# A gated state-space and channel-mix layer: a new set-up for the order of POOL's and SP's queues, D's scaling, early D products and the value weights

## The chip, the cores and the metric

One core of a Trainium2 chip runs the whole layer. The metric is the device time of one execution in microseconds (us); the time before the change is the median of three runs. All data are fp32. Engines are named as in the profile: PE is TensorE, DVE VectorE, ACT ScalarE, POOL GpSimd, SP the engine whose queue issues most transfers.

## What is computed

The input x is 4 batches of 2048 time steps of 512 channels. Six rows of modulation per batch come from a small vector c. With them the layer does this (names shortened):

```python
mod = (silu(c) @ wmod).reshape(B, 6, 1, -1)      # sa, ca, ga, sb, cb, gb
ga, gb = (sign(g) * max(abs(g), 0.25) for g in (ga, gb))
h = layernorm(x) * (1 + ca) + sa
omega = clip(softplus(h @ W_omega.T + b_omega), 1e-4, 100); d = 1 - sigmoid(h @ W_zeta.T + b_zeta)
A = omega * omega; S = 1 / (1 + DT * DT * A); F = h @ W_B.T + b_B
z, y = d*(S*z - DT*A*S*y) + F_z, d*(DT*S*z + S*y) + F_y      # over time, 64 pairs per batch
x = x + ga * (states @ C.T + h @ D.T)
h = layernorm(x) * (1 + cb) + sb
xr, xk = (mu * h + (1 - mu) * h_of_the_step_before for mu in (mu_r, mu_k))
x = x + gb * sigmoid(xr @ W_r.T) * (relu(xk @ W_k.T) ** 2 @ W_v.T)
```

## The kernel before

The sequence is cut into 32 units of 256 time steps of one batch; unit i is step range i // 4 of batch i % 4. A class `Gates` makes the inputs of the state recurrence for a unit, a function `scan` runs the recurrence for the four units of a step range together, and a class `Finish` does all the rest of a unit.

*Gates.* `load` brings x (xs, two pieces of 256 KB), `load_t` its transposed copy (xt). `norm` takes the statistics on DVE and r = 1/sqrt(var + eps) on POOL (L130). r is needed as a row on all partitions: `send` writes it to DRAM (st, L134) and `spread` reads it back broadcast (bc, L141), both on SP's queue. For the first four units `spread_now` makes the same row with a diagonal matrix and a product (L148 to L150). `project` multiplies the transposed x with the gate weights of that batch (pg, L161, one PSUM buffer), and `hand_over` scales by r on DVE (g, L169) and writes four pieces on ACT (L174). The gate weights of a batch (wgb) are the common ones scaled and centred (`shared_weights`, L512 and L517).

*Scan.* A list of closures: softening on ACT (three passes and two table loads) and on DVE (L200 to L205), eight chunk steps, joins, falls and eight state steps on DVE; then `by_batch` copies the states on ACT (L307) and moves them to y on SP's queue (L309). `take(budget)` puts the next closures of the list into the program at the place where it is called.

*Finish.* `load` brings x and its transposed copy; `shift` adds a row d0 on POOL (L337). `attend` multiplies the transposed x with D (pd, L347) and y with C (pc, L348), adds both to x on DVE (L350, L351) and takes statistics; xn is made on ACT (L363). `mix` transposes xn (L382), makes the two mixed inputs on ACT and DVE (L388, L391), first the one for the keys, with an edge added on POOL (L394). `key` (L407), `receptance` (L421) and `value` (L431) are the three big products. The D of each batch (dg) is D times the gate row ga (`d_gate`, L526, POOL), centred by `d_centre` (L533 PE, L537 DVE); C is scaled likewise (cg, L621). ga, the row of gates on all partitions, is made by `broadcast_rows`, which writes four rows to DRAM and reads them back broadcast (L505, L506, SP's queue). The value weights of a batch (wvb) are W_v scaled by gb on ACT (L670), transposed on PE (L673) and copied on ACT (L674), one piece of 128 after another.

*What sets the order.* The kernel is recorded under a manual schedule: every engine and every queue runs its own instructions in the order in which the program text issues them, each waiting for its inputs and for its buffer to be free. Tiles of pool p1 have one buffer, of p2 two, of p3 three for each tag; xs and the transposed xt share three buffers each. An instruction that waits holds everything behind it on its engine, and a transfer that waits to be issued holds its queue. The set-up is the text from the first loads to the loop over `fin`; the loop then does, for unit i, key, the gates of unit i + 8, attend and mix of unit i + 1, receptance and value, with pieces of the scan taken in between.

Of the kernel before, what the change touches and what calls it, by code (L numbers as in the profile page):

```python
# [43 lines left out]
def adaln_layer_kernel(ctx: ExitStack, tc: tile.TileContext, x, x_t, c_t, wmod, w_gate, w_b, b_gate, b_f, c_mat, d_mat,  # L44
# [64 lines left out]
    class Gates:  # L109
# [5 lines left out]

        def load(self):
            self.xs = []
            for n in range(NT):
                t = p3.tile([P, D], F32, tag="xs", name=f"xs_{self.u.tag}_{n}")
                nc.sync.dma_start(t, x[self.u.b, self.u.t0 + n * P : self.u.t0 + (n + 1) * P, :])  # L120
                self.xs.append(t)
# [21 lines left out]
        def spread_now(self, diag):  # L143
# [3 lines left out]
            for n in range(NT):  # L147
                nc.vector.tensor_scalar_mul(diag[:, ts(n, P)], ident, self.r[:, n : n + 1])  # L148
                nc.tensor.matmul(pb[:, ts(n, P)], ones, diag[:, ts(n, P)], start=True, stop=True)
# [173 lines left out]
    class Finish:  # L323
# [14 lines left out]

        def attend(self, between):
            xt, h, u = self.x, self.h, self.u  # L340
            b = u.b
            mv = p2.tile([P, NT, 2], F32, tag="mv", name=f"mv_{self.tag}")
            for n in range(NT):
                pd = ps3.tile([P, D], F32, tag="px", name=f"pd_{self.tag}_{n}")
                pc = ps3.tile([P, D], F32, tag="px", name=f"pc_{self.tag}_{n}")
                for k in range(KC):
                    nc.tensor.matmul(pd, h[:, k, ts(n, P)], dg[:, b, k, :], start=(k == 0), stop=(k == KC - 1))  # L347
                nc.tensor.matmul(pc, y_of[u.s][:, b, ts(n, P)], cg[:, b, :], start=True, stop=True)  # L348
                r = rs[:, b, u.t0 // P + n : u.t0 // P + n + 1]
                nc.vector.scalar_tensor_tensor(xt[:, n, :], pd, r, xt[:, n, :], ALU.mult, ALU.add)  # L350
# [103 lines left out]
    room = p1.tile([P, 2, KC, W], F32, tag="mixed", name="room").rearrange("p i k w -> p (i k w)")  # L454
    wraw = room[:, : KC * 4 * M].rearrange("p (k i n) -> p k i n", k=KC, i=2)
    craw = room[:, KC * 4 * M : KC * 4 * M + D]
    mag = room[:, KC * 4 * M + D :]
# [4 lines left out]
    for i, mu in enumerate((mu_r, mu_k)):  # L462
        nc.scalar.dma_start(mus[:, i, :], mu.rearrange("(k p) -> p k", p=P))
# [7 lines left out]
    gts[0].load()  # L471
    wm_ga = wmod_to(wvb[:, 1], 2)
    wm_sa = wmod_to(wvb[:, 2], 0)
    gts[0].load_t()

    dm = [
        p2.tile([P, KC // 2, D], F32, tag="y", name="dm0"),
        p1.tile([P, KC // 2, D], F32, tag="act", name="dm1"),
    ]
    for h in range(2):  # L480
        nc.scalar.dma_start(dm[h], d_mat[h * D // 2 : (h + 1) * D // 2, :].rearrange("(k p) n -> p k n", p=P))
    nc.scalar.dma_start(craw, c_mat)
# [20 lines left out]
    def broadcast_rows(dst, rows, name):  # L503
        there = dram.tile([B, D], F32, tag=name, name=name)
        nc.sync.dma_start(there, rows)  # L505
        nc.sync.dma_start(dst, there.unsqueeze(0).broadcast_to([P, B, D]))  # L506
# [17 lines left out]
    def d_gate(b):  # L524
        for h in range(2):
            nc.gpsimd.tensor_tensor(  # L526
                dg[:, b, 2 * h : 2 * h + 2, :], dm[h], ga[:, b, :].unsqueeze(1).broadcast_to([P, KC // 2, D]), ALU.mult
            )
# [12 lines left out]
    def d_rows():  # L541

        pr = ps2.tile([P, D], F32, tag="pm", name="pd0")
        for k in range(KC):
            nc.tensor.matmul(pr[:B, :], mod[:, 0, k, :], dm[k // 2][:, k % 2, :], start=(k == 0), stop=(k == KC - 1))
# [4 lines left out]
    def shift_factors():  # L550
# [7 lines left out]
        nc.vector.tensor_scalar_mul(first_f, first_f, -1.0)  # L558

# [14 lines left out]
    nc.vector.tensor_scalar_mul(mod[:, 4], mod[:, 1], 1.0 / D)  # L574
    wm_cb = wmod_to(wvb[:, 0], 4)
    gts[0].norm()
    pr = mod_rows(wm_ga, 2)
    gts[1].load()
    gts[1].load_t()
    shared_weights(0)  # L580
    sgn = p2.tile([P, D], F32, tag="r", name="sgn2")
    nc.vector.tensor_scalar(sgn[:B, :], pr[:B, :], 0.0, 2.0, ALU.is_ge, ALU.mult)
    nc.scalar.activation(mag[:B, :], pr[:B, :], AF.Abs)
# [215 lines left out]
```

## Time and profile before

| | us |
|---|---|
| median of the runs (1260.05 to 1261.03) | 1260.7 |
| the profiled execution | 1261.01 |
| its span, first to last instruction | 1259.2 |
| PE busy in the span | 1160.7 |
| DVE busy | 752.0 |
| ACT busy | 477.7 |
| POOL busy | 174.4 |

A line of the profile names the line of the kernel, the engine, the operation, and output and inputs by the program's names. In lists by time the first number is the start and the second the duration, in us; what stands in square brackets is the time that the engine idled before it and the instruction or transfer whose end came last. In lists of waits the numbers are the time in total, how often, and the longest. SPq is SP's queue, whose entries are the issue of transfers, not their landing. The clock row (PEclk) is the share of full speed that TensorE was granted.

The granted clock was 0.958 over the span. In the 300 us from the start PE is busy for 206; in each 100 us from 300 to 1200 it is busy for 100.

### The profile page before, as it was taken

Reading aid. Unit: us, or ns where it says so; the run is one execution under the profiler, and the core shown is the slowest. Engines: PE = TensorE matmul, PEld = TensorE weight load, DVE = VectorE, ACT = ScalarE, POOL = GpSimd, SP = SyncE. Lnnn points to the kernel's source line nnn. Section 1 sums busy time; section 2 is a strip of 40 time slices with the busy share of each in tenths; the row PEclk is TensorE's granted clock in tenths of the full one; section 3 lists DMA queues with packets and bytes.
Section 4 is the critical chain, followed back from the end, with each engine's and each line's share of the span. In section 5 each row is a group of like instructions: output and inputs, shape, how many; then the busy total and the mean of one; then the engine's idle time right before and its main releaser. Section 6 shows DMA issues by size and latency. Waiting matters only on the chain.

```text
span 1259.2 us, 11785 instructions
## 1 busy us (share of the span) xinstructions
PE 1160.7 (92%) x3692; PEld 674.8 (54%) x3692; DVE 752.0 (60%) x2044; ACT 477.7 (38%) x796; POOL 174.4 (14%) x254
## 2 busy tenths in 40 slices
PE   6781475899999999999999999999999999999998
PEld 2621343456655566555665555665556665555554
DVE  2557513886488647874587538863886368743332
ACT  1331534333453345434533445334533453233232
POOL 0340001111101111111111111110111011111110
PEclk9895667899999999999999999999999999999999
DMA  8565423123333333233322232323232211121100
GB/s 266 194 118 93 74 67 79 39 80 88 104 89 88 88 87 85 88 89 96 89 81 68 75 95 80 88 88 105 88 89 71 67 50 51 51 67 50 50 18 33
DMA packets 120270, 105.95 MB, mean 84 GB/s; under 512 B 15880, under 2 KB 90120, under 8 KB 119952
## 3 DMA queue, kind: packets, MB, share of 16 engines
q1 hardware_dynamic: 116064, 101.27, 29.7%
q10 hardware_dynamic: 4144, 3.94, 1.0%
q8 instruction: 29, 0.48, 0.2%
q14 instruction: 33, 0.27, 0.1%
HBM read 84.16 MB, written 16.82 MB: 80 GB/s over the span
## 4 chain that ended last, share of the span: by engine, by line
PE 86%; DVE 3%; ACT 2%; DMA 2%; issue 1%; POOL 0%; SPq 0%; DVEq 0%; ACTq 0%
PE pk_c L407 18%; PE pr_c L421 18%; PE pv_c L431 17%; PE pd_c L347 17%; PE pg L161 8%; PE pc_c L348 4%; PE pt_c L382 2%; PE pwv L673 1%; DMA bc<-st 1%; DMA xs<-in_x_dram 1%; PE pdm L533 1%; ACT wvs L670 1%; ACT wvb L674 1%; ACT f L174 0%; ACT pre L174 0%
## 5 line engine op out<-in xcount | busy, mean ns | idle before, releaser
L407 PE MATMUL pk_c<-mixed_c,wk 128*128 128x256 f32 x1024 | 228.1, 381 | 12.9 <-POOL mixed_c L394 12.9
L347 PE MATMUL pd_c<-dg,xt 128*128 128x512 f32 x512 | 232.4, 597 | 0.0
L421 PE MATMUL pr_c<-wr,mixed_c 128*128 128x512 f32 x512 | 227.0, 596 | 0.0
L431 PE MATMUL pv_c<-wvb,act_c 128*128 128x512 f32 x512 | 225.0, 592 | 0.0
L407 PEld LDWEIGHTS pk_c<-mixed_c,wk 128*128 128x128 f32 x1024 | 195.7, 191 | 53.3 <-issue 14.8
L391 DVE SCALAR_TENSOR_TENSOR mixed_c<-pt_c,prev_f,mixed_c 128x255 f32<-128x255 f32 x256 | 118.1, 482 | 122.9 <-ACT mixed_c L388 122.9
L363 ACT ACTIVATE xn_c<-x,nmr_c,rstd_c 128x512 f32<-128x512 f32 x64 | 48.6, 805 | 334.6 <-POOL nmr_c L360 334.6
L421 PEld LDWEIGHTS pr_c<-wr,mixed_c 128*128 128x128 f32 x512 | 98.2, 192 | 123.9 <-issue 123.8
L347 PEld LDWEIGHTS pd_c<-dg,xt 128*128 128x128 f32 x512 | 98.1, 192 | 110.6 <-issue 108.8
L431 PEld LDWEIGHTS pv_c<-wvb,act_c 128*128 128x128 f32 x512 | 96.7, 190 | 108.9 <-issue 106.2
L350 DVE SCALAR_TENSOR_TENSOR x<-pd_c,rs,x 128x512 f32<-128x512 f32 x64 | 47.5, 743 | 169.0 <-PE pd_c L347 168.9
L161 PE MATMUL pg<-xt,wgb 128*128 128x256 f32 x512 | 121.0, 391 | 15.4 <-DVE g L169 15.4
L388 ACT ACTIVATE mixed_c<-pt_c,mod,now_f 128x256 f32<-128x256 f32 x256 | 130.4, 561 | 11.9 <-DVE mixed_c L391 5.6
L412 ACT ACTIVATE act_c<-pk_c 128x512 f32<-128x512 f32 x64 | 38.2, 597 | 202.2 <-PE pk_c L407 202.2
L161 PEld LDWEIGHTS pg<-xt,wgb 128*128 128x128 f32 x512 | 98.7, 197 | 29.1 <-DVE g L169 15.5
L433 DVE TENSOR_TENSOR r_c<-pv_c,r_c 128x512 f32<-128x512 f32 x64 | 44.2, 690 | 90.8 <-PE pv_c L431 88.8
L359 POOL TENSOR_TENSOR rstd_c<-rstd_c,neg_half 128x2 f32<-128x2 f32 x32 | 24.6, 769 | 515.9 <-DVE nmr_c L358 515.9
L174 ACT ACTIVATE pre<-g,bias 64x256 f32<-64x256 f32 x64 | 46.8, 731 | 84.8 <-DVE g L169 84.3
L337 POOL TENSOR_TENSOR x<-x,d 128x1024 f32<-128x1024 f32 x32 | 75.6, 2362 | 2.0 <-DMA x<-in_x_dram 2.0
L348 PE MATMUL pc_c<-cg,y 128*128 128x512 f32 x128 | 66.4, 601 | 4.8 <-DVE x L350 4.8
L130 POOL TENSOR_TENSOR rs<-var,neg_half 128x2 f32<-128x2 f32 x32 | 24.9, 779 | 306.8 <-DVE var L129 292.1
L423 ACT ACTIVATE r_c<-pr_c 128x512 f32<-128x512 f32 x64 | 36.9, 588 | 51.1 <-PE pr_c L421 51.0
(119 smaller groups left out, 1029.6 us busy)
## 6 DMA issues: line engine op xcount, KB each, us to landing
xt<-in_x_t_dram SPq DMA_DIRECT2D x128, 256.0 KB, 4.6
xs<-in_x_dram SPq DMA_DIRECT2D x64, 256.0 KB, 4.6
x<-in_x_dram SPq DMA_DIRECT2D x32, 512.0 KB, 4.0
out_dram<-r_c SPq DMA_DIRECT2D x64, 256.0 KB, 2.1
wvb<-in_wmod_dram SPq DMA_DIRECT2D x5, 1024.0 KB, 9.5
y<-pre SPq DMA_DIRECT2D x64, 64.0 KB, 2.0
bc<-st SPq DMA_DIRECT2D x28, 128.0 KB, 4.7
wvb<-in_wmod_dram SPq DMA_DIRECT2D x4, 256.0 KB, 4.7
```

The source lines that it names most:

```text
L161: nc.tensor.matmul(self.pg[:, i, :], wgb[:, b, k, ts(i, P)], self.xt[:, k, :], start=(k == 0), stop=(k == KC - 1))
L174: nc.scalar.activation(dst[hs, j, :, q, :].rearrange("p l c -> p c l"), g[src, i, :].rearrange("p (c l) -> p c l", l=L), AF.Identity, bias ...
L337: nc.gpsimd.tensor_tensor(xt, xt, d0[:, self.u.b, :].unsqueeze(1).broadcast_to([P, NT, D]), ALU.add)
L347: nc.tensor.matmul(pd, h[:, k, ts(n, P)], dg[:, b, k, :], start=(k == 0), stop=(k == KC - 1))
L348: nc.tensor.matmul(pc, y_of[u.s][:, b, ts(n, P)], cg[:, b, :], start=True, stop=True)
L350: nc.vector.scalar_tensor_tensor(xt[:, n, :], pd, r, xt[:, n, :], ALU.mult, ALU.add)
L363: nc.scalar.activation(self.xn[:, n, :], xt[:, n, :], AF.Identity, bias=nmr[:, n : n + 1], scale=rstd[:, n : n + 1])
L388: nc.scalar.activation(m, pt, AF.Identity, bias=mod[:, 2, k, b : b + 1], scale=now_f[:, b, i, k : k + 1])
L391: nc.vector.scalar_tensor_tensor(m[:, 1:], pt[:, : W - 1], prev_f[:, b, i, k : k + 1], m[:, 1:], ALU.mult, ALU.add)
L407: nc.tensor.matmul(pk[:, j, :], wk[:, k, ts(2 * e + j, P)], mixed[:, 1, k, :], start=(k == 0), stop=(k == KC - 1),)
L421: nc.tensor.matmul(pr, mixed[:, 0, k, ts(n, P)], wr[:, k, :], start=(k == 0), stop=(k == KC - 1))
L431: nc.tensor.matmul(pv, act[:, k, ts(n, P)], wvb[:, u.b, k, :], start=(k == 0), stop=(k == KC - 1))
```

## The change

Only the set-up and the first two units of the loop change.

- *Loads.* The first four units' x come in one transfer each (`load_pair`, in Finish's x buffers), and the loads of wmod's columns are put into another order (sa ahead of ga). D is loaded into the tile of W_r, C and the gate sizes into a y buffer, and W_v once, early, on ACT's queue. W_r is loaded late, on POOL's queue, once D is no longer read.
- *Row of r.* `spread_now` is split: `diagonal` (DVE) can be issued earlier than the product, and uses C's tile.
- *Gate rows.* `broadcast_rows` issues its two transfers on POOL's queue. The rows of ga are computed after unit 0's gates and sent after r of unit 3.
- *D and C scaled in two parts.* `d_gate(b, h)` scales half of one batch's D, `c_gate(b)` its C. Batches 0 and 1 are scaled in the set-up ahead of r of unit 4; batches 2 and 3 around the attend and mix of unit 0.
- *D's products ahead.* `early` computes the D products of units 0 and 1 and adds them to x before the scan of the first step range is done; `attend` then has only C's product for these units.
- *Value weights.* `value_weights(jobs)` scales the next piece before it copies the last one out. Batch 0's, 1's and 2's pieces stand in the set-up, batch 3's in the loop at unit 1, after the centring of batch 3's D and after the sending of r of unit 10; these read W_v again from DRAM, each piece into an xs buffer, on SP's queue.
- *Scan.* The pieces of the first scan are taken at other places; the second scan starts in the loop at unit 0, after unit 7's gates, instead of ahead of the loop.

On POOL the order is now r of units 0 to 3, the gate rows' transfers, D and C of batches 0 and 1, r of unit 4, the transfers of d0's row, r of unit 5, the factors, the shifts of units 0 and 1, and on. On SP's queue st of unit 4 stands ahead of the loads of unit 5's x, its transposed copy, and the x and transposed x of unit 0's Finish; st of unit 10 stands ahead of the four pieces of W_v. On DVE the additions of the early D products stand ahead of chunk step 5 (unit 0) and of the last three falls (unit 1).

The functions, as a diff:

```diff
+        def load_pair(self):
+
+            t = p3.tile([P, NT, D], F32, tag="x", name=f"xs_{self.u.tag}")
+            u = self.u
+            nc.sync.dma_start(t, x[u.b, u.t0 : u.t0 + W, :].rearrange("(n p) d -> p n d", p=P))
+            self.xs = [t[:, n, :] for n in range(NT)]
...
+        def diagonal(self):
+            self.diag = cg[:, self.u.b, :W]
+            for n in range(NT):
+                nc.vector.tensor_scalar_mul(self.diag[:, ts(n, P)], ident, self.r[:, n : n + 1])
+
+        def spread_now(self):
 
             self.bc = p2.tile([P, W], F32, tag="bc", name=f"bc_{self.u.tag}")
             pb = ps3.tile([P, W], F32, tag="px", name=f"pb_{self.u.tag}")
             for n in range(NT):
-                nc.vector.tensor_scalar_mul(diag[:, ts(n, P)], ident, self.r[:, n : n + 1])
-                nc.tensor.matmul(pb[:, ts(n, P)], ones, diag[:, ts(n, P)], start=True, stop=True)
+                nc.tensor.matmul(pb[:, ts(n, P)], ones, self.diag[:, ts(n, P)], start=True, stop=True)
...
+        def direct(self, n):
+
+            u = self.u
+            pd = ps3.tile([P, D], F32, tag="px", name=f"pd_{self.tag}_{n}")
+            for k in range(KC):
+                nc.tensor.matmul(pd, self.h[:, k, ts(n, P)], dg[:, u.b, k, :], start=(k == 0), stop=(k == KC - 1))
+            return pd
+
+        def add_direct(self, n, pd):
+            u, xt = self.u, self.x[:, n, :]
+            r = rs[:, u.b, u.t0 // P + n : u.t0 // P + n + 1]
+            nc.vector.scalar_tensor_tensor(xt, pd, r, xt, ALU.mult, ALU.add)
+
+        def early(self):
+
+            for n in range(NT):
+                self.add_direct(n, self.direct(n))
+            self.has_direct = True
+
+        has_direct = False
+
         def attend(self, between):
-            xt, h, u = self.x, self.h, self.u
-            b = u.b
+            xt, u = self.x, self.u
             mv = p2.tile([P, NT, 2], F32, tag="mv", name=f"mv_{self.tag}")
             for n in range(NT):
-                pd = ps3.tile([P, D], F32, tag="px", name=f"pd_{self.tag}_{n}")
+                pd = None if self.has_direct else self.direct(n)
                 pc = ps3.tile([P, D], F32, tag="px", name=f"pc_{self.tag}_{n}")
-                for k in range(KC):
-                    nc.tensor.matmul(pd, h[:, k, ts(n, P)], dg[:, b, k, :], start=(k == 0), stop=(k == KC - 1))
-                nc.tensor.matmul(pc, y_of[u.s][:, b, ts(n, P)], cg[:, b, :], start=True, stop=True)
-                r = rs[:, b, u.t0 // P + n : u.t0 // P + n + 1]
-                nc.vector.scalar_tensor_tensor(xt[:, n, :], pd, r, xt[:, n, :], ALU.mult, ALU.add)
+                nc.tensor.matmul(pc, y_of[u.s][:, u.b, ts(n, P)], cg[:, u.b, :], start=True, stop=True)
+                if pd is not None:
+                    self.add_direct(n, pd)
...
+    wraw = p1.tile([P, KC, 2, 2 * M], F32, tag="xn", name="wraw")
     for i, src in enumerate((w_gate, w_b)):
         nc.scalar.dma_start(wraw[:, :, i, :], src.rearrange("(k p) n -> p k n", p=P))
...
+    dm = wr
+    room = p2.tile([P, B, W], F32, tag="y", name="room").rearrange("p b w -> p (b w)")
+    craw, mag = room[:, :D], room[:, D:]
...
-    gts[0].load()
-    wm_ga = wmod_to(wvb[:, 1], 2)
+    nc.scalar.dma_start(dm, d_mat.rearrange("(k p) n -> p k n", p=P))
+    nc.scalar.dma_start(craw, c_mat)
+    for i, mu in enumerate((mu_r, mu_k)):
+        nc.scalar.dma_start(mus[:, i, :], mu.rearrange("(k p) -> p k", p=P))
+    wn = p1.tile([P, KC, D], F32, tag="mixed", name="wn")
+    nc.scalar.dma_start(wn, w_v.rearrange("(k p) n -> p k n", p=P))
+
+    gts[0].load_pair()
     wm_sa = wmod_to(wvb[:, 2], 0)
     gts[0].load_t()
-
-    dm = [
-        p2.tile([P, KC // 2, D], F32, tag="y", name="dm0"),
-        p1.tile([P, KC // 2, D], F32, tag="act", name="dm1"),
-    ]
-    for h in range(2):
-        nc.scalar.dma_start(dm[h], d_mat[h * D // 2 : (h + 1) * D // 2, :].rearrange("(k p) n -> p k n", p=P))
-    nc.scalar.dma_start(craw, c_mat)
+    gts[1].load_pair()
+    wm_ga = wmod_to(wvb[:, 1], 2)
+    gts[1].load_t()
+    gts[2].load_pair()
+    gts[2].load_t()
...
-        nc.sync.dma_start(there, rows)
-        nc.sync.dma_start(dst, there.unsqueeze(0).broadcast_to([P, B, D]))
+        nc.gpsimd.dma_start(there, rows)
+        nc.gpsimd.dma_start(dst, there.unsqueeze(0).broadcast_to([P, B, D]))
...
+    def d_gate(b, h):
+        nc.gpsimd.tensor_tensor(
+            dg[:, b, 2 * h : 2 * h + 2, :], dm[:, 2 * h : 2 * h + 2, :], ga[:, b, :].unsqueeze(1).broadcast_to([P, KC // 2, D]), ALU.mult
+        )
+
+    def c_gate(b):
+        nc.gpsimd.tensor_tensor(cg[:, b, :], craw, ga[:, b, :], ALU.mult)
...
+    def value_weights(jobs):
+
+        parts = []
+
+        def scaled(b, k):
+            if b == B - 1:
+                t = src = p3.tile([P, D], F32, tag="xs", name=f"wvs_{b}_{k}")
+                nc.sync.dma_start(src, w_v[ts(k, P), :])
+            else:
+                t, src = p2.tile([P, D], F32, tag="r", name=f"wvs_{b}_{k}"), wn[:, k, :]
+            nc.scalar.mul(t, src, gb[:, k, b : b + 1])
+            return t
+
+        def turned(b, k, t):
+            pt = ps2.tile([P, KC, P], F32, tag="pt", name=f"pwv_{b}_{k}")
+            for e in range(KC):
+                nc.tensor.transpose(pt[:, e, :], t[:, ts(e, P)], ident)
+            return pt
+
+        for j, (b, k) in enumerate(jobs):
+            if j == 0:
+                parts.append(scaled(b, k))
+            pt = turned(b, k, parts[j])
+            if j + 1 < len(jobs):
+                parts.append(scaled(*jobs[j + 1]))
+            nc.scalar.copy(wvb[:, b, :, ts(k, P)], pt)
```

The set-up's order after the change, whole:

```python
pr = mod_rows(wm_ca, 1)
row = mod_row(pr, 1, 1.0)
mod_cols(row, 1, mod[:, 1])
nc.vector.tensor_scalar_mul(mod[:, 4], mod[:, 1], 1.0 / D)
gts[0].norm()
wm_cb = wmod_to(wvb[:, 0], 4)
gts[3].load_pair()
shared_weights(0)
shared_weights(1)
gts[0].diagonal()
shared_weights(2)
pr = mod_rows(wm_sa, 0)
row = mod_row(pr, 0, 0.0)
gts[0].spread_now()
mod_cols(row, 0, mod[:, 0])
gts[1].norm()
pb = ps2.tile([P, 2, B], F32, tag="pt", name="pbias")
for i in range(2):
    for k in range(KC):
        nc.tensor.matmul(pb[:, i, :], wraw[:, k, i, :], mod[:, 0, k, :], start=(k == 0), stop=(k == KC - 1))
nc.vector.tensor_add(bias, pb, bcol.unsqueeze(2).broadcast_to([P, 2, B]))
gts[0].project()
gts[1].diagonal()
gts[2].norm()
gts[0].hand_over()
pr = mod_rows(wm_ga, 2)
gts[2].diagonal()
sgn = p2.tile([P, D], F32, tag="r", name="sgn2")
nc.vector.tensor_scalar(sgn[:B, :], pr[:B, :], 0.0, 2.0, ALU.is_ge, ALU.mult)
nc.scalar.activation(mag[:B, :], pr[:B, :], AF.Abs)
nc.vector.tensor_scalar_max(mag[:B, :], mag[:B, :], GATE_MIN)
nc.vector.scalar_tensor_tensor(mag[:B, :], sgn[:B, :], 1.0, mag[:B, :], ALU.subtract, ALU.mult)
gts[3].norm()
broadcast_rows(ga, mag[:B, :], "rows2")
gts[3].load_t()
wm_sb = wmod_to(wvb[:, 1], 3)
wm_gb = wmod_to(wvb[:, 2], 5)
gts[4].load()
gts[4].load_t()
gts[1].spread_now()
gts[1].project()
gts[3].diagonal()
gts[1].hand_over()
shared_weights(3)
gts[2].spread_now()
gts[2].project()
gts[2].hand_over()
for b in range(2):
    d_gate(b, 0)
    d_gate(b, 1)
    c_gate(b)
gts[3].spread_now()
gts[3].project()
gts[4].norm()
gts[4].send()
gts[5].load()
gts[5].load_t()
fin[0].load()
gts[3].hand_over()
d_rows()
side += scan(0)
take(0.1)
nc.scalar.dma_start(wk, w_k.rearrange("(k p) n -> p k n", p=P))
d_centre(0)
gts[5].norm()
gts[5].send()
gts[4].spread()
take(7)
pr = mod_rows(wm_cb, 4)
row4 = mod_row(pr, 4, 1.0)
pr = mod_rows(wm_sb, 3)
row3 = mod_row(pr, 3, 0.0)
d_centre(1)
mod_cols(row4, 4, mod[:, 3])
mod_cols(row3, 3, mod[:, 2])
take(3.5)
pr = mod_rows(wm_gb, 5)
row5 = mod_row(pr, 5, 0.0)
mod_cols(row5, 5, gb)
gsgn = const.tile([P, KC, B], F32, name="gsgn")
nc.vector.tensor_scalar(gsgn, gb, 0.0, 2.0, ALU.is_ge, ALU.mult)
nc.scalar.activation(gb, gb, AF.Abs)
nc.vector.tensor_scalar_max(gb, gb, GATE_MIN)
nc.vector.scalar_tensor_tensor(gb, gsgn, 1.0, gb, ALU.subtract, ALU.mult)
shift_factors()
gts[4].project()
take(3)
gts[4].hand_over()
fin[1].load()
gts[5].spread()
fin[0].shift()
fin[1].shift()
jobs = [(b, k) for b in range(B) for k in range(KC)]
value_weights(jobs[:4])
fin[0].early()
take(4.5)
gts[5].project()
take(2)
gts[5].hand_over()
value_weights(jobs[4:8])
gts[6].load()
gts[6].load_t()
take(5)
gts[6].norm()
gts[6].send()
fin[1].early()
value_weights(jobs[8:12])
take(100)
take(1)
gts[6].spread()
gts[7].load()
gts[6].project()
fin[0].attend(lambda: None)
d_gate(2, 0)
gts[6].hand_over()
gts[7].norm()
gts[7].send()
gts[7].load_t()
fin[0].mix(lambda: d_gate(2, 1))
c_gate(2)
d_gate(3, 0)
d_gate(3, 1)
nc.gpsimd.dma_start(wr, w_r.rearrange("(k p) n -> p k n", p=P))
c_gate(3)
gts[7].spread()
gts[8].load()
gts[8].load_t()
gts[9].load()
```

In the loop, between key and attend (later in unit 0's turn, after mix, comes `gts[8].spread()`):

```python
    f.key()
    if i == 0:
        d_centre(2)
        gts[7].project()
        gts[7].hand_over()
        side += scan(1)
        take(0.1)
        gts[8].norm()
        gts[8].send()
    if i == 1:
        d_centre(3)
    if g1:
        g1.norm()
        g1.send()
    if i == 1:
        value_weights(jobs[3 * KC :])
        gts[i + 10].load()
```

## The prediction

> **What bounds the kernel now.** I read the page's slices first: from slice 8 on (about 250 us) TensorE is busy to nine tenths or more, and before that it is not.
>
> ```profile
> PE   6781475899999999999999999999999999999998
> PEclk9895667899999999999999999999999999999999
> ```
>
> The reader is to see that only the set-up, slices 0 to 7, has holes, and that the clock falls with them. The waits of TensorE in 0 to 250 us name the holes; the same query from 250 us to the end returns no wait at all. The three longest:
>
> ```profile
> PE pwv L673 <- ACT wvs L670: 38.4, 15, 15.4
> PE pg L161 <- DVE g L169: 15.4, 1, 15.4
> PE pk_c L407 <- POOL mixed_c L394: 12.9, 1, 12.9
> ```
>
> So every microsecond by which the set-up gets shorter, or by which a new hole opens behind it, reaches the end one for one. Two points of the chain that ended last serve as marks: the transposes of unit 1 and the D products of unit 2.
>
> ```profile
> 240.38 0.87 PE pt_c L382 x8
> ...
> 258.48 3.43 PE pd_c L347 x8
> ```
>
> From the second mark to the end are 1259.2 - 258.5 = 900.7 us, and the same products follow it in both kernels. I therefore work out when the changed kernel reaches the two marks.
>
> Next, SP's queue. A row of r (st, 1 KB, two numbers from each partition) is sent to DRAM, and what is queued behind it lands late:
>
> ```profile
> 77.39 0.37 SPq L134 DMA_DIRECT2D st<-rs  x1
> 77.85 0.89 SPq L120 DMA_DIRECT2D xs<-in_x_dram  x2
> ...
> 122.00 0.38 SPq L134 DMA_DIRECT2D st<-rs  x1
> 122.51 0.86 SPq L120 DMA_DIRECT2D xs<-in_x_dram  x2
> ```
>
> VectorE waits for these xs:
>
> ```profile
> 90.01 0.69 DVE L104 BATCH_NORM_STATS2 stats_a<-xs 128x6 f32<-128x512 f32 x1 [10.79 <-DMA xs<-in_x_dram]
> ...
> 134.55 0.69 DVE L104 BATCH_NORM_STATS2 stats_a<-xs 128x6 f32<-128x512 f32 x1 [3.50 <-DMA xs<-in_x_dram]
> ```
>
> Twice 12.1 us from issue to use, where section 6 has 4.6 as the median for xs. Last, POOL's own order:
>
> ```profile
> 52.26 0.69 POOL L130 TENSOR_TENSOR rs<-var,neg_half 128x2 f32<-128x2 f32 x1 [6.41 <-DVE var L129]
> 52.91 9.37 POOL L526 TENSOR_TENSOR dg<-dm,wvb 128x1024 f32<-128x1024 f32 x4
> 62.23 5.03 POOL L621 TENSOR_TENSOR cg<-room,wvb 128x512 f32<-128x512 f32 x4
> 67.19 9.38 POOL L526 TENSOR_TENSOR dg<-dm,wvb 128x1024 f32<-128x1024 f32 x4
> 76.67 0.69 POOL L130 TENSOR_TENSOR rs<-var,neg_half 128x2 f32<-128x2 f32 x1
> ```
>
> D's scaling costs 2.34 us a half, C's 1.26; r of unit 4 waits behind all 24 us of it.
>
> **The set-up, step by step** (my reckoning from these durations, each engine in its built order).
>
> *Up to the gate rows.* TensorE goes on from 13.8 us without the wait for wm_ga (3.5 at 13.35): three shared products of 1.72 to 19.0; the row of sa 3.43 to 22.5; its row, spread and columns to 24; bias 1.8; unit 0's gates 3.43 to 29.3; the row of ga to 32.7; sign, size and floor on ACT and VectorE to 35.2. Its new homes (the diagonals in C's tile, D in W_r's, C in y's) and the small loads moved on ACT's queue cost nothing: nobody wants those tiles before 160.
>
> *Gate rows on POOL's queue.* They stand behind the fourth r. Loads: up to unit 3's x, SP moves 7.5 MB and ACT 2.75 (w_v's early 1 MB among them); before moved 7.9 MB by 25 us, so at its rate x arrives near 32 and hides behind the stages ahead of it. Unit 3's statistics 1.8 and r 0.7 follow, to 37.8. The rows' two copies took 28.13 to 29.56 (issue to second issue) and 4.8 to land from SP's queue: 6.2 us. No row shows a copy issued by POOL. The Trainium skill, "DMA: Bandwidth & Descriptors", section "SWDGE vs HWDGE vs iDMA", has such descriptors written by software, with a first byte after about 1 us against 0.6, and its bandwidth section gives 6.15 us for 1 MB. By the row D could start at 44.1, by the page near 48; I take 46.1, nearer the row, since it is the same copy. A gain below 6.2 is excluded by the software step. D and C of two units then cost 4 x 2.34 + 2 x 1.26 = 11.9, to 58.0, and r of unit 4 leaves at 58.8 (before 77.4). D's other half, wanted only by units 2 and 3, lies later beside POOL's idle time at the first mix; The copies of d0's row, moved to POOL too, stand ahead of r of unit 5; they land near 68 and r is asked for at 73, so they hide by 5 us. W_r, issued by POOL behind the second half near 184, lands by about 194 while its user has slack until 208.
>
> *Unit 5's x* is behind that st: 58.8 + 0.5 + 12.2 = 71.5 (before 90.0). The softening stands behind its statistics in VectorE's order: 73.3 to 80.7 (7.34 as before); D's centring 2.7; two chunk steps 1.85 each; the gate columns and factors, as before about 3.3, to 91.0.
>
> *Two shifts of x* (L337, 2.36 each) now start there on POOL, both at once, ahead of chunk steps. The trace has a single such meeting:
>
> ```profile
> 139.32 2.38 DVE L299 SCALAR_TENSOR_TENSOR f<-uv,uf 128x64 f32<-128x64 f32 x1
> ```
>
> where L299 alone takes 0.22. By this row one instruction is held once: 2.2. The skill, "SBUF — State Buffer", section "Who interferes with whom", says that VectorE instructions with two SBUF inputs fully block while POOL reads SBUF: two shifts, 4.6. The chunk steps are such instructions throughout, so I take 4.6. Chunk steps 3 and 4 end at 99, and unit 4's g comes at 99.0 (before 107.2; its bc is there by 87).
>
> *Value weights pipelined.* Before a step takes 2.41 (wvs 129.34 to 131.75), four of them 9.6. ACT now needs 0.63 + 0.58 a step and hides the transposes; four end after about 5.6. They wait for unit 4's hand-over, 3.0: 102.7 to 108.3.
>
> *D's products early.* 3.43 for each of four halves, no work added, but VectorE's two additions for a unit stand ahead of chunk step 5 and of the falls, and behind TensorE's value weights. The first product after sparse work took 5.83 at L347 (172.90), so 5.6 + 3.4: VectorE idles from 99.7 to 114 and to 117.5, and likewise from 132.6 to 145 for the second unit. This wait is new; the scan is queued behind it. Then: falls 2.3, eight state steps 9.45, copies and y 6: y at 163. Before, D's products started at 172.9 with y there already.
>
> *First unit.* C's product, additions and statistics 3.6, POOL and xn to 169.6, hand-over 3.0, first half of mix 2.5: key at 175.1 (before 204.57). Key 8.9 cold, centring and unit 7's gates to 190.9, hand-over 194.6, softening on ACT 5.0 to 199.7, on VectorE 7.3 to 207.0, and only behind it unit 1's addition, statistics, a chunk step, xn: first mark at 215.3. That is 25.1 ahead of before.
>
> **Behind the first mark.** Before did the centring of unit 3 (3.45) and the last four value weights (1.8) ahead of it; that is 5.25 given back. TensorE has idled since about 200, so the restart at half clock costs 1.7 (L407's 8.90 against 6.91 is 2.0). Left: 18.1.
>
> Then the new wait. The last value weights read w_v again, from SP's queue, behind the st of unit 10. Counted from the end of the centring product: VectorE's dg 2.9, statistics to st 2.8 (219.58 to 222.39), issue 0.5, landing 12.2, ACT 0.7: first transpose at +19.1. The fourth piece needs the first one's buffer (three of them): +20.3, then issue 0.4, the ordinary 4.6, ACT 0.7: transposes end at +27.2 against 1.8 of work. Queued behind it on TensorE are the products of unit 2; ACT's scaling holds xn of unit 2 as well. Nothing covers it: 25.4, and a cold restart 2.4, is 27.8. From below, were the pieces to land in 4.6, it is 20.2; from above, with busy queues, some 31.
>
> Sum: 27.8 - 18.1 = 9.7 later at the second mark. Span 1259.2 + 9.7 = 1268.9; the profiled execution is 1.8 above its span and 0.3 above the median: 1270.4 against 1260.7.
>
> **Rivals.** *The clock stays granted* (not slower): value weights without gaps keep TensorE at full clock, so that five restarts (two D products 2.4 each, key 2.0, first mark 1.7, second mark 2.4) cost nothing: 10.9, hence 1259.5; with the shifts held once instead of twice, 1257. For it: at 142 to 146 transposes took 0.66 although gaps of 1.3 lay between. Against it: four of the five gaps are over 10 us, and after such gaps the trace is always slow. It decides from 9.7. *The w_v pieces are not held by st*: 27.8 becomes 20.2, hence 1262.8; the two 12.1 speak against it. *POOL's queue is slower than the page says*, since VectorE's two-port instructions keep it from writing descriptors: each microsecond is on the path up to the first mark; twice the 8.2 gives 1278.6. *The early products move no time*: if y were as late as in before, the whole 25.1 would go and 1295 remain; VectorE's 18.6 earlier softening speaks against that.
>
> **Chances.** Forecast 0.52 (1264 to 1277), clock 0.19, pieces not held 0.12, POOL slower 0.15, no gain 0.02. About 0.2% (2.5 us) is what a measurement of this kernel can tell from no change. Faster 0.19, within 0.11, slower 0.70. Range 1256 to 1284.
>
> **What would show it.** D's first scaling near 46 and r of unit 4 near 58; g of unit 4 near 99; VectorE idle for the early D products by some 18 and 12 us; key near 175; transposes of unit 1 near 215 with TensorE idle ahead of them; then, above all, a wait of transposes of value weights for ACT of 15 to 20 us behind unit 3's centring, with the w_v pieces 12 us in the queue. I am wrong if that wait is under 15 us, or if the first mark comes before 205.

## The result and the profile after

| | median, us | spread of runs | profiled execution, span | clock |
|---|---|---|---|---|
| before | 1260.4 | 1260.0 to 1263.0 (6) | 1261.0, 1259.2 | 0.958 |
| after | 1269.1 | 1263.9 to 1269.5 (6) | 1268.3, 1266.5 | 0.956 |

The ratio over all runs is 1.0059, 95% interval 1.0041 to 1.0076: slower by 0.4 to 0.8% (the medians alone would give 1.0069; one run of the six, 1263.9, is shorter than the rest). In the spans of the two profiled executions it is 7.3 us. First the slices of the page, as before the change:

```profile
PE   7945565579999999999999999999999999999998
PEclk9977767879999999999999999999999999999999
```

The set-up still has its holes, and slice 8, full before, now shows a 7 with a clock of 7. The waits of TensorE in the first 290 us (us in total, times, longest):

```profile
PE pwv L608 <- ACT wvs L602: 46.1, 9, 19.3
PE pt_c L411 <- ACT xn_c L392: 19.7, 4, 15.5
PE pc_c L377 <- DMA y<-pre: 9.3, 1, 9.3
```

The 15.4 for g and the 12.9 for mixed are down to 0.7 and 3.6; the longest is a new one, 19.3. The chain that ended last shows its place (start, us, what):

```profile
214.95 1.76 PE pt_c L411 x7
...
235.38 3.45 PE pdm L565 x8
...
244.58 0.38 SPq L141
244.96 0.04 issue
245.01 12.25 DMA wvs<-in_w_v_dram
...
258.11 1.13 PE pwv L608 x4
...
259.29 2.61 DMA wvs<-in_w_v_dram
...
263.87 5.20 PE pd_c L355 x8
```

The first mark comes at 214.2 (its first transpose) in place of 240.4, 26 ahead. Then the chain leaves TensorE, passes VectorE and POOL to st on SP (L141), a scatter (256 single numbers sent to DRAM), and stands 12.25 in the load of w_v behind it; the fourth piece takes 2.61 more. The second mark, 258.5 before, is at 263.9: 5.4 behind. Its first product is cold, 5.20 against 3.43; that is nearly all of the rest of the 7.3. Cold means here that TensorE runs at a lower granted clock after a pause: 0.50 from 263.7 to 267.0, where it was 1.00 from 220 to 235; the same products stood at 1.00 before the change (258.4 to 261.7).

Now the set-up's own stations. The gate rows, on POOL:

```profile
38.04 0.73 POOL L535 DMA_DIRECT2D rows<-room  x1
44.21 0.58 POOL L536 DMA_DIRECT2D wvb<-rows  x1 [5.43 <-DMA rows<-room]
49.24 4.66 POOL L555 TENSOR_TENSOR dg<-wr,wvb 128x1024 f32<-128x1024 f32 x2 [4.45 <-DMA wvb<-rows]
60.93 0.71 POOL L137 TENSOR_TENSOR rs<-var,neg_half 128x2 f32<-128x2 f32 x1
```

From issue to D's scaling are 11.2 us; of these the write of 8 KB alone has 6.2. r of unit 4 (last line) still comes 16 us ahead of before. The two shifts of x, and what VectorE did beside them:

```profile
93.05 4.63 POOL L348 TENSOR_TENSOR x<-x,d 128x1024 f32<-128x1024 f32 x2
93.13 2.30 DVE L590 TENSOR_SCALAR first_f<-first_f 128x32 f32<-128x32 f32 x1 [1.94 <-POOL first_f L589]
95.35 2.76 DVE L242 TENSOR_TENSOR uv<-new,pre 128x384 f32<-128x384 f32 x1
```

The same instruction L242 takes 0.56 at 99.39; each shift held one instruction to its end. And VectorE's additions of the early D products:

```profile
115.55 0.75 DVE L361 SCALAR_TENSOR_TENSOR x<-pd_c,rs,x 128x512 f32<-128x512 f32 x1 [13.74 <-PE pd_c L355]
118.90 0.75 DVE L361 SCALAR_TENSOR_TENSOR x<-pd_c,rs,x 128x512 f32<-128x512 f32 x1 [2.60 <-PE pd_c L355]
...
140.59 0.75 DVE L361 SCALAR_TENSOR_TENSOR x<-pd_c,rs,x 128x512 f32<-128x512 f32 x1 [6.77 <-PE pd_c L355]
143.94 0.75 DVE L361 SCALAR_TENSOR_TENSOR x<-pd_c,rs,x 128x512 f32<-128x512 f32 x1 [2.60 <-PE pd_c L355]
```

25.7 us in which VectorE waits, with the scan queued behind it, and 3.0 for the additions themselves.

**The question.** The prediction's account is this: the gain up to the first mark is real and is spent on one wait behind it, w_v behind st. The rival that the profile suggests beside it is that the gain should have been far larger, and that the early products and the rows hold it. Each can be undone alone.

### The profile page after: what moved, and what is told of

It is laid out like the page before. It is cut to its first block, busy times and chain, and to the rows that moved or that the text cites. A ratio compares the mean times of both kernels' runs of the same rounds, so it can differ in the third digit from the quotient of the medians.

```text
span 1266.5 us, 11792 instructions
## 1 busy us (share of the span) xinstructions
PE 1161.3 (92%) x3692; PEld 675.6 (53%) x3692; DVE 747.1 (59%) x2044; ACT 477.4 (38%) x796; POOL 176.8 (14%) x259
## 4 chain that ended last, share of the span: by engine, by line
PE 81%; DMA 1%; DVE 0%; ACT 0%; POOL 0%; issue 0%; SPq 0%; DVEq 0%; ACTq 0%
PE pv_c L460 17%; PE pk_c L436 17%; PE pr_c L450 17%; PE pd_c L355 16%; PE pg L172 7%; PE pc_c L377 4%; PE pt_c L411 2%; DMA wvs<-in_w_v_dram 1%; PE pdm L565 0%; DVE dg L569 0%; PE pwv L608 0%; ACT xn_c L392 0%; ACT wvs L602 0%; DVE stats_a L104 0%; POOL rs L137 0%; DVE r_c L462 0%
## 5 line engine op out<-in xcount | busy, mean ns | idle before, releaser
L137 POOL TENSOR_TENSOR rs<-var,neg_half 128x2 f32<-128x2 f32 x32 | 24.5, 764 | 295.2 <-DVE var L136 295.2
L608 PE MATMUL pwv<-ident,wvs 128*128 128x128 f32 x64 | 14.9, 393 | 46.1 <-ACT wvs L602 46.1
```

## The experiments

Each ratio is against the kernel before, run on the same chip; the marks are the first transpose of unit 1 and the first D product of unit 2, in us, from the timelines (the chains put them up to 0.2 later). The spans follow the second mark within 3 us, save in c2 and c3, which load no w_v behind the first mark and where one more wait follows it. A span is that of one profiled execution, and the experiments ran on other chips than the first two rows; the kernel before alone spans 1256.2 to 1261.2 over all of its runs. What a step is worth is therefore given by ratios (0.001 is 1.26 us), and the marks tell where it comes from.

| kernel | ratio, 95% | first mark | second mark | span |
|---|---|---|---|---|
| before | 1 | 240.2 | 258.3 | 1259.2 |
| after | 1.0059, 1.0041 to 1.0076 | 214.2 | 263.7 | 1266.5 |
| e1, w_v ahead of st | 0.9941, 0.9927 to 0.9955 | 212.4 | 246.3 | 1248.3 |
| e4, w_v on ScalarE's queue | 1.0033, 1.0020 to 1.0045 | 213.8 | 258.7 | 1260.7 |
| e2, rows on SP's queue | 1.0009, 1.0001 to 1.0017 | 206.5 | 254.4 | 1257.7 |
| e3, no early products | 0.9889, 0.9876 to 0.9903 | 194.8 | 240.5 | 1243.3 |
| c1, these three | 0.9704, 0.9690 to 0.9717 | 188.5 | 219.8 | 1221.1 |
| c2, gates first | 0.9733, 0.9720 to 0.9746 | 191.3 | 212.8 | 1221.1 |
| c3, softening behind | 0.9693, 0.9676 to 0.9710 | 183.0 | 214.2 | 1222.1 |
| b1, before + pipelined | 0.9885, 0.9871 to 0.9898 | 225.2 | 243.3 | 1244.3 |
| b2, before + rows on POOL | 1.0000, 0.9991 to 1.0008 | 239.8 | 257.9 | 1258.8 |
| e7, additions late | 0.9919, 0.9907 to 0.9932 | 200.5 | 247.2 | 1249.5 |
| e8, rows on ScalarE's queue | 1.0097, 1.0083 to 1.0111 | 219.8 | 269.3 | 1271.7 |

**e1: the w_v pieces ahead of st.**

```diff
-            g1.send()
+            if i != 1:
+                g1.send()
         if i == 1:
             value_weights(jobs[3 * KC :])
+            g1.send()
             gts[i + 10].load()
```

> Against the changed kernel only the order of two steps on SP's queue differs: the four pieces of w_v for the last value weights go out ahead of the scatter st of unit 10, no longer behind it. Theory 1 (the net loss is the wait behind st): the wait of the transposes for ScalarE, 19.3 us in the changed kernel, falls to some 5, and the second batch of it (fourth piece) goes too; about 15 us less, 1269.1 - 15 = 1254, faster than before (1260.4) by 0.5%. Rival (the stretch is bound by the other work of units 1 and 2 there, xn and softening, and the wait only shows in another place): the wait is renamed, 1265 to 1269.

Theory 1 holds: by the ratios the order of two issues is worth 14.9 us (1.0059 to 0.9941, some 12 to 18 with both intervals; 18.2 between the two profiled spans), and with it alone the change wins. Of the 19.3 in the changed kernel, 6.2 passed before the pieces were issued at all (238.8 to 245.0, while st waited for its r), and 12.3 from there to their use. The wait isn't wholly gone (3.6 + 2.3 + 0.3): the pieces share three buffers with the x of the gates.

**e4: the pieces on ScalarE's queue**, st where it was (`nc.scalar.dma_start(src, w_v[ts(k, P), :])` in place of `nc.sync`).

> Against the changed kernel only the queue of the four w_v pieces differs: ScalarE's in place of SP's; the scatter st of unit 10 stays where it is on SP's. It tells what in st holds the pieces. If it is the order of one queue: a piece lands in 2 to 5 us from its issue in place of 12.3, and the wait of 19.3 shrinks by 7 to 10; 1259 to 1262. If it is that the scatter's packets occupy the transfer engines that all queues share: 10 to 12 us from issue to landing as before, 1267 to 1270. A third outcome: ScalarE's own order puts the issue later or earlier than SP's 245.0; then the landing from issue still tells the two apart.

The timeline of e4, last two pieces (ACTq and SPq issue, ACT scales):

```profile
243.02 0.34 ACTq L599 DMA_DIRECT2D wvs<-in_w_v_dram  x1
244.44 0.38 SPq L141 DMA_DIRECT2D st<-rs  x1
...
245.67 0.72 ACT L602 ACTIVATE wvs<-wvs,gb 128x512 f32<-128x512 f32 x1 [1.54 <-DMA wvs<-in_w_v_dram]
245.81 0.33 ACTq L599 DMA_DIRECT2D wvs<-in_w_v_dram  x1
...
256.97 0.72 ACT L602 ACTIVATE wvs<-wvs,gb 128x512 f32<-128x512 f32 x1 [10.10 <-DMA wvs<-in_w_v_dram]
```

The piece issued 1.4 ahead of st is in use 2.7 after its issue; the one issued 1.4 behind it, on another queue, takes 11.2. Two loads of x, issued on SP's queue from 244.93 to 247.99, don't explain it: such loads land after 4.6 in the median. So the order of one queue isn't what holds the piece: behind the scatter a load of another queue is held as well. By its landing this is the second outcome, of the engines that all queues share; by its time it lies between, since three pieces slipped in ahead of st. What the scatter does to the others stays open. It is itself slow, by the row of issues of the changed kernel (KB, median us to landing):

```profile
st<-rs SPq DMA_DIRECT2D x28, 1.0 KB, 10.2
```

But it doesn't fill the engines: from 245 to 255 us in the changed kernel their mean busy share is 0.18, at 24 GB/s.

**e2: gate rows and d0's row on SP's queue** (`nc.sync` in both copies of broadcast_rows).

> Against the changed kernel the gate rows and d0's row go out on SP's queue again in place of POOL's. Theory 1: the rows took 11.2 us on POOL's queue where SP's took about 8 in the kernel before, but on SP's queue they stand in order with loads and scatters; D's scaling starts some 3 earlier, d0's row some 3 to 5 earlier and ScalarE and TensorE no longer wait 11 and 5 us for it; r of unit 4 some 3 earlier, first mark 3 to 5 earlier, 1264 to 1266. Rival (the rows are off the path up to the first mark, which the early products and the clock set): within 1 us of the changed kernel, 1268 to 1270. If SP's order holds the rows behind a scatter, later than on POOL's: over 1270.

```profile
35.34 0.34 SPq L535 DMA_DIRECT2D rows<-room  x1
36.77 0.36 SPq L536 DMA_DIRECT2D wvb<-rows  x1
...
41.90 4.67 POOL L555 TENSOR_TENSOR dg<-wr,wvb 128x1024 f32<-128x1024 f32 x2 [4.00 <-DMA wvb<-rows]
```

D's scaling starts 7.3 earlier: 2.7 because the rows no longer stand behind r of unit 3 on POOL, 4.6 because they take 6.6 in place of 11.2. The first mark is 7.8 earlier, the span 8.8 shorter; by the ratios it is 6.3 us, more than theory 1 asked, and the rival falls. d0's row didn't get quicker (issued at 66.3, read back at 74.3; it was 61.6 and 71.5).

**b2: the kernel before with the rows on POOL's queue** (`nc.gpsimd` in both copies).

> The kernel before with one part of the change alone: the gate rows and d0's row on POOL's queue. Theory 1 (POOL's queue itself costs 4 to 5 for a small write and its read back, wherever it stands): D's scaling starts 4 to 7 later and with it r of the later units, 4 to 9 more, 1263 to 1268. Rival (only the changed order puts the rows on the path; here POOL has slack): within 1 of the kernel before.

No change at all: the rival. Its rows:

```profile
29.73 0.72 POOL L505 DMA_DIRECT2D rows<-room  x1 [12.32 <-DVE diag L148]
31.96 0.58 POOL L506 DMA_DIRECT2D wvb<-rows  x1 [1.51 <-DMA rows<-room]
```

The same write takes 2.2 from POOL's queue here, 6.2 in the changed kernel. What differs is the traffic. The DMA engines' busy tenths in 40 slices, first of the changed kernel from 30 to 50 us, then of b2 from 28 to 36, each with its row of the issues (KB, us to landing):

```profile
DMA  9999999999999999999999999952101959987000
...
rows<-room POOLq DMA_DIRECT2D x1, 8.0 KB, 5.9
```

```profile
DMA  9999864231110001000000000099095994996995
...
rows<-room POOLq DMA_DIRECT2D x1, 8.0 KB, 1.9
```

In the changed kernel the engines are full from 30 to 44, with x and the modulation weights that SP went on loading because the rows were no longer in its order; in b2 they are nearly idle at the write.

**e8: the rows on ScalarE's queue**, amid the same loads (`nc.scalar` in both copies).

> The changed kernel with the gate rows and d0's row on ScalarE's queue in place of POOL's, issued while the same loads of x and of the modulation weights are under way. On POOL's queue the 8 KB write took 6.2 from issue to the next issue in the changed kernel, and 2.2 in the kernel before with POOL's queue. Theory 1 (the loads under way occupy the transfer engines; the kind of queue is nothing): 4 to 6 from issue to landing on ScalarE's queue too. Rival (the kind of queue, with VectorE busy beside it): 1 to 2 as on SP's queue in the kernel before. Time within 4 of the changed kernel either way, since ScalarE waits in its own order for the write.

```profile
35.42 0.52 ACTq L535 DMA_DIRECT2D rows<-room  x1
...
39.89 0.37 ACTq L536 DMA_DIRECT2D wvb<-rows  x1
...
47.62 4.67 POOL L555 TENSOR_TENSOR dg<-wr,wvb 128x1024 f32<-128x1024 f32 x2 [9.40 <-DMA wvb<-rows]
```

A queue that isn't POOL's, and the write still takes 4.5 and the read back 7.7: 12.2 in all, against 6.6 from SP's, where the loads stand behind the rows. Theory 1 holds for the traffic. The time is 4.8 over the changed kernel by the ratios, a little outside the 4: ScalarE stands in its own order behind both writes (6.1 and 20.8 us of waiting), and the first softening on it starts at 77.3 in place of 51.4.

**e3: no early products** (both calls of early() left out; the products are made in attend, as before).

> Against the changed kernel the products of D of the first two units are made again behind the states, with the others, and not ahead of them. Theory 1 (the early products cost VectorE's idle 13.7 + 2.6 and 6.8 + 2.6, with the scan queued behind): states and y come some 20 us earlier, and up to 14 us of products come back on TensorE, part of it beside y's way; first mark 5 to 15 us earlier, 1254 to 1264. Rival (the early products fill time that TensorE has anyway, and the states are not what the first unit waits for): later by the products' own time, 3.4 x 4 = 13.7 and a cold start, 1275 to 1284.

The largest single effect: 21.4 us by the ratios (23.2 by the profiled spans), more than theory 1 gave. The copies of the last state to y on ScalarE, first after, then e3:

```profile
156.23 2.03 ACT L318 COPY pre<-f 128x256 f32<-128x256 f32 x4 [8.22 <-DVE f L309]
```

```profile
131.76 2.06 ACT L318 COPY pre<-f 128x256 f32<-128x256 f32 x4 [2.44 <-DVE f L309]
```

y comes 24.5 earlier. What the early products buy is small: from those copies to the first unit's transposes are 11.5 us with them and 14.2 without, since the first half's products now lie beside y's way to TensorE. So they cost 24.5 and return 2.7 on the first unit. I expected much of the 14 us of TensorE to come back on the path; nearly none did.

**e7: unit 0's products early, their additions late.** It parts TensorE's share from VectorE's.

```diff
-    fin[0].early()
+    fin[0].held = [fin[0].direct(n) for n in range(NT)]
...
-    fin[1].early()
...
-                pd = None if self.has_direct else self.direct(n)
+                pd = self.held[n] if self.held else None if self.has_direct else self.direct(n)
```

> The changed kernel with the first unit's D products still made early on TensorE, but held in PSUM and added by VectorE only behind the states; the second unit's products are not early. It parts the two halves of the early step: TensorE's work and VectorE's two additions in the scan's order. Theory 1 (what costs is that VectorE, and the scan queued behind it, waits for the products): as without early products, 1244.8 on a chip where the kernel before gives 1258.8, and up to 3 less, since 11.4 in place of 14.1 lie between the last state and the first transpose; ratio 0.987 to 0.990. Rival (TensorE's and ScalarE's time in the set-up is what costs, the products being cold): some 5 to 10 of the 23 come back, ratio 0.993 to 0.998.

Neither: 0.9919 lies between. The copies start at 140.36, 15.9 ahead of the changed kernel and 8.6 behind e3. The 8.6 has its line, in VectorE's timeline:

```profile
122.30 0.69 DVE L180 TENSOR_TENSOR g<-pg,bc 128x512 f32<-128x512 f32 x1 [12.63 <-PE pg L172]
```

In e3 this wait for unit 5's gate products is 5.1, so it makes 7.5 of the 8.6. With the additions gone, the products still stand ahead of pg in TensorE's order, and VectorE's next scan step stands behind its g. So about two thirds of the 24.5 goes with VectorE's additions and the second unit's products, one third with the first unit's products in TensorE's order. How the two thirds divide isn't shown by any run.

**b1: the kernel before with the pipelined value weights alone.**

```diff
-        for k in range(KC):
+        def scaled(k):
...
+            return t
+
+        t = scaled(0)
+        for k in range(KC):
...
+            if k + 1 < KC:
+                t = scaled(k + 1)
```

> The kernel before with one part of the change alone: the value weights pipelined. By the prediction a batch of four takes 5.6 in place of 9.6. Theory 1 (a batch lies on the path up to the first mark): one to two batches count, 4 to 8 less, 1251 to 1255. Rival (the batches lie beside the scan, which VectorE sets): within 1 of the kernel before, 1258 to 1260.

By the ratio 14.5 us shorter: theory 1's cause, at twice its size. I had put one or two batches on the path; the timeline of TensorE (the first line of a batch has two of its four parts, and the same products stand at 129.34 and 172.90 before) has all four ahead of the first unit's products:

```profile
128.63 1.97 PE L677 MATMUL pwv<-ident,wvs 128*128 128x128 f32 x8 [15.78 <-ACT wvs L670]
...
156.58 2.21 PE L677 MATMUL pwv<-ident,wvs 128*128 128x128 f32 x8 [0.50 <-ACT wvs L670]
158.58 5.45 PE L347 MATMUL pd_c<-dg,xt 128*128 128x512 f32 x8
```

Before, VectorE idled 29.59 ahead of its first addition: the value weights, not the scan, held the first unit.

```profile
178.85 0.75 DVE L350 SCALAR_TENSOR_TENSOR x<-pd_c,rs,x 128x512 f32<-128x512 f32 x1 [29.59 <-PE pd_c L347]
```

One part of the change alone beats the kernel before by more than the whole loses.

**c1: e1, e2 and e3 together**, on two chips. One line differs from e1: st stands behind the load of unit 11's x too, not only behind the pieces of w_v.

> The changed kernel with three of its steps undone at once: rows on SP's queue, the products of D of two units behind the states again, the w_v pieces ahead of the scatter st. Theory 1 (three separate prices, each on the path): against the changed kernel, about 1266 on this chip by its ratio to the kernel before, the single runs gave -5.9, -21.5 and -15.7; they add up to -43 and give 1223 (1220 to 1227). Rival (the waits cover one another; with the first mark 30 earlier, TensorE meets the next wait): half of the second and third are kept, 1235 to 1244.

> The run with three steps undone once more, for its profile. Theory 1: the first mark (transposes of unit 1) some 31 ahead of the changed kernel's 214.2, at about 184; the wait for the pieces some 4 + 2, unit 2's first product near 214; 1222 to 1226 where the kernel before gives 1260.

0.9717 (0.9701 to 0.9733) and 0.9704: the single differences of ratio from the changed kernel (-0.0118, -0.0050, -0.0170) add up to -0.0338, that is 0.9721. Three prices, nearly independent: 42.6 us as a sum, 43 and 45 measured. The marks came 4 to 6 later than expected (188.5, 219.8), though the time is right.

**c2: D and C scaled for all four early, so that the last value weights need no load** (with e2 and e3):

```diff
     gts[4].send()
+    for b in range(2, B):
+        d_gate(b, 0)
+        d_gate(b, 1)
+        c_gate(b)
...
-    value_weights(jobs[8:12])
+    value_weights(jobs[8:16])
```

> Rows on SP's queue and no early products, as in the run with three steps undone; here the last value weights wait for no load at all: D and C are scaled for all four on POOL ahead of unit 5's statistics (12 us of POOL while it and VectorE wait), so that the gate rows' place is free and the last four value weights come from the w_v that is still there, beside the states. Theory 1 (what is left behind the first mark is the wait for the pieces, some 10 us with its cold start): 8 to 10 below the run with three steps undone, 1213 to 1217. Rival (the four value weights beside the states hold the falls' last copy on ScalarE, or POOL's 12 us hold unit 5's r, by as much as they save): within 2 of that run, or above it.

The rival's time, but not for its reason alone: the second mark is 7.0 ahead of c1, and behind it TensorE waits 4.3 for unit 2's x and runs the next products cold, 8.76 against 7.03. The first mark is 2.8 later. The saved wait was handed on.

**c3: in c2, unit 7's softening behind unit 1's additions.**

> The run with the gates first, and there unit 7's softening and the start of the second scan put behind unit 1's additions on VectorE. Theory 1 (in that run TensorE waits 9.2 for VectorE's x of unit 1, which stands behind the softening, 7.3, and restarts cold): 8 to 10 less, 1214 to 1218 where the kernel before gives 1260. Rival (the second scan, begun later, is then late for its first unit, or the next unit's addition waits in its place, 4.3 in that run): within 3 of that run.

```profile
190.76 9.87 PE L460 MATMUL pv_c<-wvb,act_c 128*128 128x512 f32 x16 [3.31 <-ACT r_c L452]
...
201.83 3.69 PE L436 MATMUL pk_c<-mixed_c,wk 128*128 128x256 f32 x16 [1.21 <-DVE r_c L462]
```

The first mark comes 8.3 earlier, and the gain is lost in the next stage: receptance, on ScalarE and VectorE, now stands behind the softening. Beside c1 on the same chip, 0.9693 and 0.9704, it can't be told apart. Against c2, which ran on another chip, it is 5.0 us less by the ratios (0.9733 to 0.9693, some 2 to 8 with both intervals), between theory 1 and the rival. The profiles show none of it: the second mark is 1.4 later than c2's and the span 1.0 longer, c2's profiled execution being the shortest of its five. So the 8 to 10 of theory 1 didn't come, and whether a smaller gain is left isn't settled. All of c1, c2 and c3 beat both kernels by about 3%.

## Why the prediction was right

**The mechanism held.** First mark 215.3 forecast, 214.2 measured; the first transposes behind the wait for w_v +19.1 after the centring product's end, measured +19.3 (238.8 to 258.1); slower by 0.8%, measured 0.6%. The w_v pieces took 12.3 from issue to use, as the two xs of before had (12.1). The sum of 9.7 came out at 7.3, nearly all of it by these terms: the fourth piece landed in 2.6 in place of the ordinary 4.6 (-2.0, transposes done at +25.0, not +27.2); the cold restart at the second mark cost 1.8, not 2.4 (-0.6); the first mark came 1.1 sooner; the cold restart at the first mark cost about 1.2 more than its 1.7 (2.3 for the transposes, in two pieces, where 0.87 is the hot time, and 4.90 for the gates where it is 3.46).

**Two errors of the set-up cancelled.** The rows took 11.2, not 8.2, so D's scaling came at 49.2 (46.1 forecast), r of unit 4 at 60.9 (58.1), unit 5's statistics at 74.2 (71.5), g of unit 4 at 101.1 (99.0). The other way, the early products of the second unit kept VectorE 9.4, not 12.4, and y was used at 160.2, not 163. So the 215.3 is as close as it is by luck, with its middle 3 us off on both sides.

**Of the rules weighed.** Two shifts held VectorE by 2.1 and 2.2, about 4.3 in all: the doubled value that I took from the Trainium skill, "SBUF — State Buffer", "Who interferes with whom", was right, and the 2.2 of the single row too small. The trace before had more such meetings than the single one that I named. Beside D's scaling, which starts on POOL at 52.91 with 2.34 for each instruction, it has

```profile
52.98 4.73 DVE L148 TENSOR_SCALAR diag<-ident,rs 128x128 f32<-128x128 f32 x2
```

where the same two took 0.48 at 45.88: two instructions held, each for one of POOL's. This line would have decided for the double. For the copies the skill's rule on descriptors written by software ("DMA: Bandwidth & Descriptors", "SWDGE vs HWDGE vs iDMA") gave a D at 48; measured 49.2, but not by that mechanism: in b2 the same queue had 0.8 more than SP's (2.2 against 1.4), and the other 4 came with full DMA engines, as 4.5 did from ScalarE's queue in e8. The rival *POOL's queue is slower* thus has its size right in part and its cause wrong; a price copied from an idle moment doesn't hold amid loads.

**The rivals.** *The clock stays granted*: no; the restarts are in the trace (unit 0's early D products 8.87 where two of 3.43 would be hot, the second unit's 7.74, key 9.48, gates 5.11, and the second mark). *The pieces are not held by st*: no in this kernel, and e1 shows what it was worth; I gave it 7.6 where st behind the pieces gives 14.9, because I let the pieces still be issued behind st and only land sooner. *d0's row hides by 5*: its read back was issued at 71.5, not landed at 68; ScalarE's next row waited for the write, and TensorE 5.1 for that. (The write was issued at 61.6, beside the st of unit 4 at 61.7; whether that held it wasn't tested.) r of unit 5, asked at 76.1, wasn't held.

**What the prediction didn't see.** It had the early products in its sum, rightly, as a wait with the scan behind it, but never set the change with them against the change without them. Before, the first unit waited for value weights and VectorE had 29.6 us to spare. With pipelining alone 15.8 of that is left (b1, at 164.15), and with all of the change save the early products 5.2 (e3, at 137.09). So little slack was left just where the change put two waits into the scan. The gain was there: by the ratios the early products held back 21 us, the order of st and w_v 15, the rows 6, each alone, and 45 together (c1). A slip beside it: from the second mark to the end of before are 1000.7 us, not the 900.7 that the prediction gives; only the difference of the marks enters its sum.

## What to carry to other kernels

Price each part of a change alone, against the bound that the other parts leave: work that fills a hole while one engine is the bound becomes a wait in the order of the next. When a small transfer is taken out of a queue, ask what the queue now sends in its place, and whether that is in the way. Put a scatter of single numbers behind the loads that matter soon, not ahead of them; a load issued behind it on another queue was as late (11.2 us in e4).

## What the runs showed of the hardware that was not expected

- A scatter of 256 single numbers (1 KB) held a transfer of another queue: 11.2 us from issue to use for a 256 KB load on ScalarE's queue issued 1.4 behind it, 2.7 for one issued 1.4 ahead (e4), while the DMA engines' mean busy share was low (0.18 in the changed kernel).
- An 8 KB write landed in 1.9 us with idle DMA engines (b2) and 5.9 with full ones (after), from the same queue; 4.5 to the next issue from ScalarE's with full ones (e8).
- An instruction of VectorE that is held by one of POOL's need not have two tensors as inputs: first_f, a TENSOR_SCALAR of 128x32, took 2.30 beside a shift, where it had taken 0.18 before the change (at 113.55).
